# A last output and the next first tokens carried across a loop's back edge, with hints for its branch

## The chip, the core and the metric

The kernel runs on one core of one Trainium2 chip. The metric is the time of one execution on the device in microseconds (us), taken as the median of several runs. Before the change it is 9271.71 us, the median of 3 runs (9268.06 to 9273.82).

The engines are called as in the profile: PE is TensorE (PEld its weight loads), DVE is VectorE, ACT is ScalarE, POOL is GpSimd, SP is SyncE, which issues most DMA transfers. Each engine runs its own instruction stream, and each has its own copy of a loop's branch. A name with a q, such as PEldq, is the sequencer of that engine, which carries out branches, register loads and waits. L784 is line 784 of the kernel's file; the lines of the kernel before and after the change differ.

## The reference, cut to what matters

```
x = x + xattn(layernorm(x), ctx)         # 4 x 1024 tokens of 1024 values
h = layernorm(x).reshape(4096, 1024)
probs = softmax(h @ gate_w)              # 8 experts
topk_w, topk_idx = top_k(probs, 2)       # every token goes to 2 experts
topk_w = topk_w / sum(topk_w)
# for each expert e, on the tokens routed to it:
#   g = silu(h @ w1[e]) * (h @ w3[e])    # 1024 -> 3584
#   o = g @ w2[e]                        # 3584 -> 1024
out = x + sum over the 2 experts of topk_w * o
```

All of it is in float32. There are 4096 tokens and so 8192 pairs of token and expert, about 1024 for each of the 8 experts.

## The kernel before

**The parts.** The first 537 us hold the cross attention, the norms and the routing. They write the normed tokens to DRAM (`h_d`), write x into the output (`of`), put the ids and weights of each expert's tokens in a list (`id_d`), and fill a small table of *runs*: the expert of each run (`run_e`), its first slot in the list (`run_s`), its kind (`run_k`), and the number of runs (`run_n`). With this input there are 8 runs, one for each expert, of 3 blocks each, with widths of 328 to 360 tokens.

**The loop.** `tc.For_i(0, n_run)` at L784 goes over the runs; the number is read from memory. Its body reads the run's table entries into registers and jumps with `tc.Switch(kind, 13)` (L788) into one of 13 unrolled bodies, `run(i, ex, s0, blocks, width)` (L664), one for each kind in `RUNS`. At the end of a body every engine waits for its own work and for the others, and branches back. The order of PE's instructions in a body is the order in which the program is written (`manual_schedule`); a scheduler orders the other engines.

**One block** is `width` tokens, cut in `split` parts of up to 128 rows, the third part being 72 to 104 rows here.

- *Phase 1*: 14 steps `i2`, in each a tile of w1 and one of w3, 1 MB each, streamed by SP into three buffers (`load`, tag `w`). The products follow a scheme with seven half-size products p1 to p7 in place of eight: `weight_sums` (L573 to L577, four DVE operations) makes the sums of the weights' quarters, `token_sums` (L587) those of the tokens, the matmuls at L735 make the seven products (56 for one tile) in four PSUM banks, and `combine` (L599: a copy by ACT at L608, DVE at L610, 612, 613, 614) puts them together to c1 or c3. Then silu and a product give `g`.
- *Phase 2*: 4 column quarters q of w2, with matmuls at L766 and `combine` to `y`.
- *Tokens out* (`tokens_out`): for each part two transposes of y (L697) into PSUM and one accumulation into `acc` by DVE (L701); at the last quarter the three rows tiles are scattered to the output by POOL's indirect DMA (L707). `acc` is gathered from the output at the start of phase 2. The output of a quarter waits in a list `late` and is carried out after the first part of the next quarter's matmuls, or after the first tile of the next block; the last one of a run is carried out at the end of the body (`while late`, L779).
- *Tokens in* (`tokens_in`, L668): a copy of the ids, 24 transposes of the gathered rows (L679) in six PSUM tiles, copied to `x` by ACT (L687) and DVE (L685) in turn, and the token sums. It stands at the head of a run for its first block, and after the combine of quarter q = 1 for the next block of the same run.
- *Ahead of time*: `load_rows` (ids by SP, three gathers by POOL at L638) fetches the next block's rows at the start of a block. In the last block `load_first(i + 1)` (L749) does so for the next run, and loads its first two weight tiles to buffers of their own, w1a and w3a.

So a run of the loop ends with the last quarter's combine, its transposes, accumulation and scatters, and the next one begins, behind the branch and the switch, with the 24 transposes of its first tokens, four weight sums of w1a and then the first matmul at L735.

Of the kernel before, what the change touches and what calls it, by code (L numbers as in the profile page):

```python
# [18 lines left out]
P = 128  # L19
# [14 lines left out]
def kernel(  # L34
# [489 lines left out]


    with ExitStack() as st:
        fst = st.enter_context(tc.tile_pool(name="fst", bufs=1))
        wp = st.enter_context(tc.tile_pool(name="wp", bufs=3))
        ap = st.enter_context(tc.tile_pool(name="ap", bufs=1))
        hp = st.enter_context(tc.tile_pool(name="hp", bufs=1))  # L530
# [10 lines left out]
        HK = KD // 2  # L541
        NI = KM // 2


# [15 lines left out]

        def weight_sums(t, kn, halves):

            n = kn // 2
            if halves:
                v = t[:, :kn, :].rearrange("p (i h) c -> p i h c", h=2)
                lo, hi = v[:, :, 0, :], v[:, :, 1, :]
            else:
                lo, hi = t[:, :n, :], t[:, n:kn, :]
            a11, a21 = lo[:, :, :P], lo[:, :, P:]
            a12, a22 = hi[:, :, :P], hi[:, :, P:]  # L570
            s = wp.tile([P, 3, HK, P], F32, tag="s", name="ws")
            s1, s2, s4 = s[:, 0, :n, :], s[:, 1, :n, :], s[:, 2, :n, :]
            nc.vector.tensor_tensor(s1, a21, a22, ALU.add)  # L573
            nc.vector.tensor_tensor(s2, s1, a11, ALU.subtract)  # L574
            nc.vector.tensor_tensor(s4, a12, s2, ALU.subtract)  # L575
            s3 = a21
            nc.vector.tensor_tensor(s3, a11, a21, ALU.subtract)  # L577
            return dict(p1=a11, p2=a12, p3=s4, p4=a22, p5=s1, p6=s2, p7=s3)

# [18 lines left out]

        def combine(pp, n, tag):  # L599

            def pair(t):
                return t[:, : 2 * n].rearrange("p (a b) -> p a b", b=n)

            def twice(v):
                return v.unsqueeze(1).to_broadcast([P, 2, n])

            p1s = gp.tile([P, n], F32, tag="p1s", name="p1s")
            nc.scalar.copy(p1s, pp[0][:, :n])  # L608
            c = gp.tile([P, 4, n], F32, tag=tag, name=tag)
            nc.vector.tensor_tensor(c[:, 0:2, :], pair(pp[1]), twice(p1s), ALU.add)  # L610
            vu = gp.tile([P, 2, n], F32, tag="vu", name="vu")
            nc.vector.tensor_tensor(vu, pair(pp[2]), twice(c[:, 1, :]), ALU.add)  # L612
            nc.vector.tensor_tensor(c[:, 1:3, :], pair(pp[3]), vu, ALU.add)  # L613
            nc.vector.tensor_tensor(c[:, 3, :], pp[2][:, :n], vu[:, 1, :], ALU.add)
            return c

# [32 lines left out]
        w1a = fst.tile([P, KD, QW], F32, name="w1a")  # L649
        w3a = fst.tile([P, KD, QW], F32, name="w3a")  # L650

        def load_rows(s0):
# [5 lines left out]
        def load_first(i):  # L658
            ex = expert(i)
            load_rows(first_slot(i))  # L660
            weights(w1a, w1f, ex, 0, KD, 0)
            weights(w3a, w3f, ex, 0, KD, 0)

        def run(i, ex, s0, blocks, width):  # L664
            n = width // 2
            split = [min(P, width - c) for c in range(0, width, P)]

            def tokens_in():  # L668

                ids = ip.tile([P, RT, IDW], I32, tag="ids", name="ids")  # L670
                nc.vector.tensor_copy(ids, ids0)
                rd = ip.tile([P, RT], I32, tag="rd", name="rd")
                nc.vector.tensor_copy(rd, rd0)
                x = hp.tile([P, HK, 7 * n], F32, tag="x", name="x")
                for s, r in enumerate(split):
                    for h in range(2):
                        pt = pst.tile([P, N], F32, tag="pt", name="pt_h")
                        for k in range(HK):
                            nc.tensor.transpose(  # L679
                                pt[:, ts(k, r)], rows[s][:r, ts(HK * h + k, P)], ident[:r, :r]  # L680
                            )
                        src = pt[:, : HK * r].rearrange("p (a b) -> p a b", b=r)
                        dst = x[:, :, ds((B11 + 2 * h) * n + s * P, r)]
                        if h % 2:
                            nc.vector.tensor_copy(dst, src)  # L685
                        else:
                            nc.scalar.copy(dst, src)  # L687
                xv = x.rearrange("p k (q c) -> p k q c", q=7)
                token_sums(xv, n)
                return ids, rd, xv  # L690

            def tokens_out(ids, acc, q, y):
                yv = y.rearrange("p (d h) c -> p d (h c)", h=2)
                for s, r in enumerate(split):
                    pt = pst.tile([P, N], F32, tag="pt", name="pt_y")
                    for d in range(2):
                        nc.tensor.transpose(  # L697
                            pt[:r, ts(d, P)], yv[:, d, ds(s * P, r)], ident
                        )
                    part = acc[s][:r, ts(q, QW)]  # L700
                    nc.vector.scalar_tensor_tensor(  # L701
                        part, pt[:r, :QW], ids.bitcast(F32)[:r, s, 1:2], part,
                        ALU.mult, ALU.add,
                    )
                if q == DQ - 1:
                    for s, r in enumerate(split):
                        nc.gpsimd.indirect_dma_start(  # L707
                            out=of,
                            out_offset=bass.IndirectOffsetOnAxis(
                                ap=ids[:r, s, 0:1], axis=0  # L710
                            ),
                            in_=acc[s][:r, :],
                            in_offset=None,
                            bounds_check=T - 1,
                            oob_is_err=False,
                        )

            late = []
            now = tokens_in()
            for b in range(blocks):  # L720
                ids, rd, x = now
                last = b == blocks - 1
# [3 lines left out]
                for i2 in range(NI):  # L726
                    cs = []
                    for wf, wa, tag in ((w1f, w1a, "c1"), (w3f, w3a, "c3")):
                        t = load(wf, ex, 0, KD, i2 * QW) if b or i2 else wa
                        left = weight_sums(t, KD, False)  # L730
                        pp = banks()
                        for p in ORDER if b or i2 else EARLY:
                            bk, half = BANK[p]
                            for k in range(HK):
                                nc.tensor.matmul(  # L735
                                    pp[bk][:, ts(half, n)], left[p][:, k, :],
                                    x[:, k, RIGHT[p], :],
                                    start=(k == 0), stop=(k == HK - 1),
                                )
                        cs.append(combine(pp, n, tag))  # L740
                        while late:
                            late.pop(0)()
                    c1, c3 = cs
                    nc.scalar.activation(c1, c1, AF.Silu)  # L744
                    nc.vector.tensor_tensor(g[:, i2, B11 : B22 + 1, :], c1, c3, ALU.mult)  # L745
                    token_sums(g[:, i2, :, :], n)

                if last:
                    load_first(i + 1)  # L749
                acc = [  # L750
                    ap.tile([P, D], F32, tag=f"acc{s}", name="acc") for s in range(len(split))
                ]
                for s, r in enumerate(split):
                    gather(acc[s][:r, :], of, rd, s, r)
                for q in range(DQ):
                    pp = banks()
                    i2 = 0
                    for kn in W2K:
# [14 lines left out]
                        while late:  # L773
                            late.pop(0)()
                    y = combine(pp, n, "y")
                    late.append(lambda a=ids, c=acc, d=q, e=y: tokens_out(a, c, d, e))
                    if q == 1 and not last:
                        now = tokens_in()
            while late:  # L779
                late.pop(0)()  # L780

        load_first(0)
        n_run = nc.values_load(run_n, min_val=1, max_val=NRUN)
        with tc.For_i(0, n_run) as i:  # L784
            ex = expert(i)
            s0 = first_slot(i)
            kind = nc.values_load(run_k[:, ds(i, 1)], min_val=0, max_val=len(RUNS) - 1)
            for k in tc.Switch(kind, len(RUNS)):  # L788
                with tc.manual_schedule(engines={ENG.PE}):
                    run(i, ex, s0, *RUNS[k])  # L790


# [26 lines left out]
```

## Time and profile before

| | |
|---|---|
| median of 3 runs | 9271.71 us (9268.06 to 9273.82) |
| the profiled execution | 9277.28 us, its span 9275.4 us |
| mean granted clock of PE | 0.977 |
| PE busy | 8865.5 us, 96%, 59428 matmuls and transposes |
| PEld busy | 8665.9 us, 93% |
| DVE busy | 5115.8 us, 55%, 10003 instructions |
| ACT, POOL busy | 694.4 us (7%), 406.0 us (4%) |
| DMA | 1236.36 MB, mean 133 GB/s |
| matmuls of phase 1 (L735) | 3285.3 + 2571.8 us |
| matmuls of phase 2 (L766) | 2031.6 + 1619.6 us |
| transposes of tokens in (L679) | 98.3 us busy, 272.7 us idle just before them |
| weight tiles of 1 MB | 848, median 5.1 us from issue to landing |
| scatters to the output (L707) | 72, three a block |

The table gives busy time of each engine in one profiled execution. "Idle before" of a group of instructions is the time in which its engine did nothing just ahead of them. The span is what the profiler saw of the execution from its first to its last instruction; the execution's own time is 1.9 us longer. Granted clock is the share of TensorE's full clock that the throttle gave.

### The profile page before, as it was taken

How to read it: one execution, taken by the hardware profiler on the slowest of the kernel's cores; microseconds unless marked ns; L12 is line 12 of the kernel's file. 1: busy time of each engine (PE TensorE's matmuls, PEld its weight loads, DVE VectorE, ACT ScalarE, POOL GpSimd, SP SyncE). 2: the span in 40 equal slices, each digit the busy share in tenths (PEclk: the TensorE clock that was granted, in tenths of full speed). 3: DMA queues.
4: the chain of work that ended last, by engine and by line, in shares of the span. 5: the costliest groups of instructions: out<-in, count | busy, mean ns of one | idle time of the engine just before them, and what ended most of it. 6: DMA issues, size and time to landing. Idle time of an engine off the chain costs nothing. (4 is left out here: it accounts for less than half of the span.)

```text
span 9275.4 us, 139976 instructions
## 1 busy us (share of the span) xinstructions
PE 8865.5 (96%) x59428; PEld 8665.9 (93%) x59429; DVE 5115.8 (55%) x10003; ACT 694.4 (7%) x1524; POOL 406.0 (4%) x494
## 2 busy tenths in 40 slices
PE   8979998999989999899989999899998999989999
PEld 5569998999989999899989999899998999989999
DVE  5655654655645555556546556465564565555654
ACT  3300000000000000000000000000000000000000
POOL 2310000000000000000000000000000000000000
PEclk9979999999999999999999999999999999999999
DMA  3234444344433444344434434444443344434343
GB/s 132 109 123 145 138 144 141 125 147 130 157 118 118 143 131 138 119 136 138 141 128 135 139 121 138 132 132 146 137 147 120 125 140 135 141 117 141 124 134 127
DMA packets 1116668, 1236.36 MB, mean 133 GB/s; under 512 B 34848, under 2 KB 1077280, under 8 KB 1115872
## 3 DMA queue, kind: packets, MB, share of 16 engines
q1 hardware_dynamic: 1079424, 1114.54, 37.1%
q0 software_dynamic: 31952, 107.24, 3.3%
q8 instruction: 500, 8.19, 0.4%
q10 hardware_dynamic: 4496, 3.97, 0.1%
q14 instruction: 296, 2.42, 0.1%
HBM read 1155.26 MB, written 70.65 MB: 132 GB/s over the span
## 5 line engine op out<-in xcount | busy, mean ns | idle before, releaser
L735 PE MATMUL ps<-x,wt 128*128 128x168 f32 (+3 forms) x20992 | 3285.3, 309 | 0.0
L735 PEld LDWEIGHTS ps<-x,wt 128*128 128x128 f32 x20992 | 3123.4, 190 | 0.0
L735 PE MATMUL ps<-x,ws 128*128 128x168 f32 (+3 forms) x16128 | 2571.8, 309 | 0.0
L735 PEld LDWEIGHTS ps<-x,ws 128*128 128x128 f32 x16128 | 2411.8, 190 | 0.0
L766 PE MATMUL ps<-g,wt 128*128 128x168 f32 (+3 forms) x10752 | 2031.6, 310 | 0.0
L573 DVE TENSOR_TENSOR ws<-wt 128x512 f32<-128x512 f32 (+1 forms) x1040 | 693.8, 667 | 2206.3 <-DMA wt<-in_L_ffn_w_dram 2123.3
L766 PEld LDWEIGHTS ps<-g,wt 128*128 128x128 f32 x10752 | 1693.4, 191 | 0.0
L766 PE MATMUL ps<-g,ws 128*128 128x168 f32 (+3 forms) x8064 | 1619.6, 310 | 0.0
L766 PEld LDWEIGHTS ps<-g,ws 128*128 128x128 f32 x8064 | 1299.0, 191 | 0.2 <-DVE y L610 0.2
L610 DVE TENSOR_TENSOR c<-ps,p1s 128x352 f32<-128x352 f32 (+3 forms) x672 | 346.7, 516 | 1045.1 <-PE ps L735 1016.1
L574 DVE TENSOR_TENSOR ws<-ws,wt 128x512 f32<-128x512 f32 (+1 forms) x1040 | 692.4, 666 | 30.2
L577 DVE TENSOR_TENSOR wt<-wt 128x512 f32<-128x512 f32 (+1 forms) x1040 | 685.3, 659 | 0.0
L575 DVE TENSOR_TENSOR ws<-wt,ws 128x512 f32<-128x512 f32 (+1 forms) x1040 | 684.3, 658 | 0.0
L608 ACT COPY p1s<-ps 128x168 f32<-128x168 f32 (+3 forms) x768 | 228.5, 298 | 5319.3 <-PE ps L766 2881.0
L744 ACT ACTIVATE c<-c 128x672 f32<-128x672 f32 (+3 forms) x336 | 261.6, 778 | 2559.5 <-DVE c L613 2543.4
L613 DVE TENSOR_TENSOR c<-ps,vu 128x352 f32<-128x352 f32 (+3 forms) x672 | 344.6, 513 | 43.2 <-PE ps L735 36.2
L679 PE MATMUL pt_h<-ident,rows 128*128 128x128 f32 (+4 forms) x576 | 98.3, 319 | 272.7 <-DVE ws L573 128.4
L612 DVE TENSOR_TENSOR vu<-ps,c 128x352 f32<-128x352 f32 (+3 forms) x672 | 342.2, 509 | 17.5 <-PE ps L735 17.5
L679 PEld LDWEIGHTS pt_h<-ident,rows 128*128 128x128 f32 (+4 forms) x576 | 74.9, 169 | 295.0 <-issue 240.3
L745 DVE TENSOR_TENSOR g<-c,c 128x672 f32<-128x672 f32 (+3 forms) x336 | 294.1, 875 | 11.3
L638 POOL DMA_INDIRECT rows<-h_d,rd x75 | 78.1, 1042 | 4180.1 <-DVE ws L574 4136.0
L707 POOL DMA_INDIRECT out_dram<-acc,ids x72 | 74.0, 1028 | 4136.6 <-DVE acc L701 3929.3
(165 smaller groups left out, 3073.3 us busy)
## 6 DMA issues: line engine op xcount, KB each, us to landing
wt<-in_L_ffn_w_dram SPq DMA_DIRECT2D x848, 1024.0 KB, 5.1
wt<-in_L_ffn_w_dram SPq DMA_DIRECT2D x192, 768.0 KB, 4.7
xt<-in_x_dram SPq DMA_DIRECT2D x32, 512.0 KB, 4.4
out_dram<-x SPq DMA_DIRECT2D x32, 512.0 KB, 2.9
h_d<-hn SPq DMA_DIRECT2D x32, 512.0 KB, 2.6
w1a<-in_L_ffn_w_dram SPq DMA_DIRECT2D x9, 1024.0 KB
w3a<-in_L_ffn_w_dram SPq DMA_DIRECT2D x9, 1024.0 KB, 11.9
cx<-in_ctx_dram SPq DMA_DIRECT2D x4, 1024.0 KB, 9.9
```

The lines of the kernel that those rows point to most:

```text
L573: nc.vector.tensor_tensor(s1, a21, a22, ALU.add)
L574: nc.vector.tensor_tensor(s2, s1, a11, ALU.subtract)
L575: nc.vector.tensor_tensor(s4, a12, s2, ALU.subtract)
L577: nc.vector.tensor_tensor(s3, a11, a21, ALU.subtract)
L608: nc.scalar.copy(p1s, pp[0][:, :n])
L610: nc.vector.tensor_tensor(c[:, 0:2, :], pair(pp[1]), twice(p1s), ALU.add)
L612: nc.vector.tensor_tensor(vu, pair(pp[2]), twice(c[:, 1, :]), ALU.add)
L613: nc.vector.tensor_tensor(c[:, 1:3, :], pair(pp[3]), vu, ALU.add)
L735: nc.tensor.matmul(pp[bk][:, ts(half, n)], left[p][:, k, :], x[:, k, RIGHT[p], :], start=(k == 0), stop=(k == HK - 1),)
L744: nc.scalar.activation(c1, c1, AF.Silu)
L745: nc.vector.tensor_tensor(g[:, i2, B11 : B22 + 1, :], c1, c3, ALU.mult)
L766: nc.tensor.matmul(pp[bk][:, ts(half, n)], left[p][:, k, :], g[:, i2, RIGHT[p], :], start=(i2 == 0 and half == 0), stop=(i2 == NI - 1 and ...
```

## The change

- **Last output.** The last block's quarter q = 3 is combined into a tile `y1` that lives outside the loop, and the body ends there. A function `leftover()` does the tokens out of `y1` with ids kept in `ids1`: the next run puts it first in its `late` list, so it is carried out after the first weight tile's matmuls and combine, and once more behind the loop. It always takes three full tiles of 128 rows; the ids of rows beyond the block's width are put out of range (`beyond`), so that the scatter leaves them out. Ahead of the first run `acc` and `y1` are set to zero and `ids1` to an id out of range (`NONE`).
- **First tokens.** `tokens_in` stands after q = 1 of every block, the last one too, and once ahead of the loop. It always transposes three tiles of 128 rows. `x` lives outside the loop, is stored as two halves of contiguous tokens, and its sums (`xs`) are made by `token_factors(n)`, four DVE operations: in place for the blocks of a run, at the head of a run for its first block. The copies of ids (`take_ids`) are made at the head of each block.
- **First weight sums.** The sums of w1a are made in the last block of the run before, after its `tokens_in`, into `s1a` outside the loop; ahead of the loop for the first run.
- **Buffers.** `acc` lives outside the loop; `y` has one buffer in place of two.
- **Hints.** `For_i` gets `hint_engines` for the five engines.

The diff, cut to its core (`factors` and `weight_sums` now return the same products as before, with the buffer of the sums given from outside if wanted; `combine` writes into a given tile):

```diff
+        s1a = fst.tile([P, 3, HK, P], F32, name="s1a")
+        x = fst.tile([P, KD, XW], F32, name="x")
+        xs = fst.tile([P, HK, 3, NM], F32, name="xs")
+        ids1 = fst.tile([P, RT, IDW], I32, name="ids1")
+        nc.gpsimd.memset(ids1, NONE)
+        acc = [fst.tile([P, D], F32, name=f"acc{s}") for s in range(RT)]
+        for a in acc:
+            nc.gpsimd.memset(a, 0.0)
+        y1 = fst.tile([P, 2 * XW], F32, name="y1")
+        nc.gpsimd.memset(y1, 0.0)
...
+        def tokens_in():
+            for s in range(RT):
+                for h in range(2):
+                    pt = pst.tile([P, N], F32, tag="pt", name="pt_h")
+                    for k in range(HK):
+                        nc.tensor.transpose(
+                            pt[:, ts(k, P)], rows[s][:, ts(HK * h + k, P)], ident
+                        )
...
+        def token_factors(n):
+            b11, b12 = x[:, :HK, :n], x[:, :HK, n : 2 * n]
+            b21, b22 = x[:, HK:, :n], x[:, HK:, n : 2 * n]
+            t1, t2, t4 = (xs[:, :, j, :n] for j in range(3))
+            nc.vector.tensor_tensor(t1, b12, b11, ALU.subtract)
+            t3 = b12
+            nc.vector.tensor_tensor(t3, b22, b12, ALU.subtract)
+            nc.vector.tensor_tensor(t2, b22, t1, ALU.subtract)
+            nc.vector.tensor_tensor(t4, b21, t2, ALU.subtract)
+            return dict(p1=b11, p2=b21, p3=b22, p4=t4, p5=t1, p6=t2, p7=t3)
...
+        def leftover():
+            tokens_out(ids1, [P] * RT, DQ - 1, y1)
+
         def run(i, ex, s0, blocks, width):
...
-            late = []
-            now = tokens_in()
+            late = [leftover]
+            right = token_factors(n)
             for b in range(blocks):
-                ids, rd, x = now
+                ids, rd = take_ids()
...
-                        left = weight_sums(t, KD, False)
+                        if t is w1a:
+                            left = factors(w1a, KD, False, s1a)
+                        else:
+                            left = weight_sums(t, KD, False)
...
                 if last:
                     load_first(i + 1)
-                acc = [
-                    ap.tile([P, D], F32, tag=f"acc{s}", name="acc") for s in range(len(split))
-                ]
+                    beyond = ip.tile([P, RT], F32, tag="beyond", name="beyond")
+                    nc.vector.tensor_scalar(
+                        beyond, at, float(width), float(NONE), ALU.is_ge, ALU.mult
+                    )
+                    nc.vector.tensor_tensor(ids1[:, :, 0], beyond, ids[:, :, 0], ALU.add)
+                    nc.vector.tensor_copy(ids1[:, :, 1], ids[:, :, 1])
...
-                    y = combine(pp, n, "y")
-                    late.append(lambda a=ids, c=acc, d=q, e=y: tokens_out(a, c, d, e))
-                    if q == 1 and not last:
-                        now = tokens_in()
-            while late:
-                late.pop(0)()
+                    if last and q == DQ - 1:
+                        combine(pp, n, y1, XW)
+                        break
+                    y = gp.tile([P, 2 * XW], F32, tag="y", name="y", bufs=1)
+                    combine(pp, n, y, XW)
+                    late.append(lambda a=ids, d=q, e=y: tokens_out(a, split, d, e))
+                    if q == 1:
+                        tokens_in()
+                        if last:
+                            weight_sums(w1a, KD, False, s1a)
+                        else:
+                            right = token_factors(n)
 
         load_first(0)
+        tokens_in()
+        weight_sums(w1a, KD, False, s1a)
         n_run = nc.values_load(run_n, min_val=1, max_val=NRUN)
-        with tc.For_i(0, n_run) as i:
+        with tc.For_i(0, n_run, hint_engines=(ENG.PE, ENG.DVE, ENG.Activation, ENG.SP, ENG.Pool)) as i:
...
+        leftover()
```

In the changed kernel the matmuls stand at L776 (phase 1) and L815 (phase 2), the transposes of tokens in at L699, those of tokens out at L726 with the accumulation at L728 and the scatter at L733, and the loop at L841.

More of the change, by code (lines that the diff above doesn't have):

```diff
@@ L528 @@
         wp = st.enter_context(tc.tile_pool(name="wp", bufs=3))
-        ap = st.enter_context(tc.tile_pool(name="ap", bufs=1))
         hp = st.enter_context(tc.tile_pool(name="hp", bufs=1))
@@ L542 @@
         NI = KM // 2
+        NM = RUNS[-1][1] // 2
+        XW = RT * P
+        assert all(w // 2 <= NM and w <= XW for _, w in RUNS)
         T1, B11, B12, B21, B22, T2, T4 = range(7)
@@ L559, in load, with factors @@
             return t
-        def weight_sums(t, kn, halves):
+        def factors(t, kn, halves, s):
             n = kn // 2
@@ L568, in weight_sums @@
                 lo, hi = t[:, :n, :], t[:, n:kn, :]
[L569 to L578, printed above, removed]
+            s1, s2, s4 = (s[:, j, :n, :] for j in range(3))
+            return dict(
+                p1=lo[:, :, :P], p2=hi[:, :, :P], p3=s4, p4=hi[:, :, P:], p5=s1, p6=s2,
+                p7=lo[:, :, P:],
+            )
+        def weight_sums(t, kn, halves, s=None):
+            if s is None:
+                s = wp.tile([P, 3, HK, P], F32, tag="s", name="ws")
+            f = factors(t, kn, halves, s)
+            a11, a12, a21, a22 = f["p1"], f["p2"], f["p7"], f["p4"]
+            nc.vector.tensor_tensor(f["p5"], a21, a22, ALU.add)
+            nc.vector.tensor_tensor(f["p6"], f["p5"], a11, ALU.subtract)
+            nc.vector.tensor_tensor(f["p3"], a12, f["p6"], ALU.subtract)
+            nc.vector.tensor_tensor(a21, a11, a21, ALU.subtract)
+            return f
         RIGHT = dict(p1=B11, p2=B21, p3=B22, p4=T4, p5=T1, p6=T2, p7=T3)
@@ L597, in banks, with combine @@
             return [ps.tile([P, N], F32, tag="ps", name=f"ps{i}") for i in range(4)]
-        def combine(pp, n, tag):
+        def combine(pp, n, c, wide):
             def pair(t):
@@ L608, in combine @@
             nc.scalar.copy(p1s, pp[0][:, :n])
-            c = gp.tile([P, 4, n], F32, tag=tag, name=tag)
-            nc.vector.tensor_tensor(c[:, 0:2, :], pair(pp[1]), twice(p1s), ALU.add)
+            nc.vector.tensor_tensor(pair(c), pair(pp[1]), twice(p1s), ALU.add)
             vu = gp.tile([P, 2, n], F32, tag="vu", name="vu")
[L612 to L615, printed above, removed]
+            nc.vector.tensor_tensor(vu, pair(pp[2]), twice(c[:, n : 2 * n]), ALU.add)
+            mid = c[:, n : 2 * wide - n].rearrange("p (a b) -> p a b", b=wide - n)[:, :, :n]
+            nc.vector.tensor_tensor(mid, pair(pp[3]), vu, ALU.add)
+            nc.vector.tensor_tensor(
+                c[:, wide + n : wide + 2 * n], pp[2][:, :n], vu[:, 1, :], ALU.add
+            )
         def expert(i):
@@ L650 @@
         w3a = fst.tile([P, KD, QW], F32, name="w3a")
+        s1a = fst.tile([P, 3, HK, P], F32, name="s1a")
[8 more added lines that the diff above has]
+        nc.gpsimd.memset(y1, 0.0)
+        at_i = fst.tile([P, RT], I32, name="at_i")
+        nc.gpsimd.iota(at_i, pattern=[[P, RT]], base=0, channel_multiplier=1)
+        at = fst.tile([P, RT], F32, name="at")
+        nc.vector.tensor_copy(at, at_i)
         def load_rows(s0):
@@ L662, in load_first, with tokens_out @@
             weights(w3a, w3f, ex, 0, KD, 0)
+        def tokens_in():
[5 more added lines that the diff above has]
+                            pt[:, ts(k, P)], rows[s][:, ts(HK * h + k, P)], ident
+                        )
+                    src = pt.rearrange("p (a b) -> p a b", b=P)
+                    dst = x[:, ds(HK * h, HK), ts(s, P)]
+                    if h % 2:
+                        nc.vector.tensor_copy(dst, src)
+                    else:
+                        nc.scalar.copy(dst, src)
+        def token_factors(n):
[8 more added lines that the diff above has]
+            return dict(p1=b11, p2=b21, p3=b22, p4=t4, p5=t1, p6=t2, p7=t3)
+        def tokens_out(ids, split, q, y):
+            yv = y.rearrange("p (d c) -> p d c", d=2)
+            for s, r in enumerate(split):
+                pt = pst.tile([P, N], F32, tag="pt", name="pt_y")
+                for d in range(2):
+                    nc.tensor.transpose(pt[:r, ts(d, P)], yv[:, d, ds(s * P, r)], ident)
+                part = acc[s][:r, ts(q, QW)]
+                nc.vector.scalar_tensor_tensor(
+                    part, pt[:r, :QW], ids.bitcast(F32)[:r, s, 1:2], part, ALU.mult, ALU.add
+                )
+            if q == DQ - 1:
+                for s, r in enumerate(split):
+                    nc.gpsimd.indirect_dma_start(
+                        out=of,
+                        out_offset=bass.IndirectOffsetOnAxis(ap=ids[:r, s, 0:1], axis=0),
+                        in_=acc[s][:r, :],
+                        in_offset=None,
+                        bounds_check=T - 1,
+                        oob_is_err=False,
+                    )
+        def leftover():
+            tokens_out(ids1, [P] * RT, DQ - 1, y1)
         def run(i, ex, s0, blocks, width):
@@ L666, in run, with take_ids @@
             split = [min(P, width - c) for c in range(0, width, P)]
-            def tokens_in():
+            def take_ids():
                 ids = ip.tile([P, RT, IDW], I32, tag="ids", name="ids")
@@ L673, in tokens_in @@
                 nc.vector.tensor_copy(rd, rd0)
[L674 to L716, printed above, removed]
@@ L718, in run @@
-            late = []
-            now = tokens_in()
+                return ids, rd
+            late = [leftover]
+            right = token_factors(n)
             for b in range(blocks):
-                ids, rd, x = now
+                ids, rd = take_ids()
                 last = b == blocks - 1
@@ L736, in run @@
                                     pp[bk][:, ts(half, n)], left[p][:, k, :],
-                                    x[:, k, RIGHT[p], :],
+                                    right[p][:, k, :],
                                     start=(k == 0), stop=(k == HK - 1),
                                 )
-                        cs.append(combine(pp, n, tag))
+                        c = gp.tile([P, 4 * n], F32, tag=tag, name=tag)
+                        combine(pp, n, c, 2 * n)
+                        cs.append(c)
                         while late:
@@ L744, in run @@
                     nc.scalar.activation(c1, c1, AF.Silu)
-                    nc.vector.tensor_tensor(g[:, i2, B11 : B22 + 1, :], c1, c3, ALU.mult)
+                    nc.vector.tensor_tensor(
+                        g[:, i2, B11 : B22 + 1, :].rearrange("p a b -> p (a b)"), c1, c3,
+                        ALU.mult,
+                    )
                     token_sums(g[:, i2, :, :], n)
@@ L749, in run @@
                     load_first(i + 1)
-                acc = [
-                    ap.tile([P, D], F32, tag=f"acc{s}", name="acc") for s in range(len(split))
-                ]
+                    beyond = ip.tile([P, RT], F32, tag="beyond", name="beyond")
+                    nc.vector.tensor_scalar(
+                        beyond, at, float(width), float(NONE), ALU.is_ge, ALU.mult
+                    )
+                    nc.vector.tensor_tensor(ids1[:, :, 0], beyond, ids[:, :, 0], ALU.add)
+                    nc.vector.tensor_copy(ids1[:, :, 1], ids[:, :, 1])
                 for s, r in enumerate(split):
@@ L774, in run @@
                             late.pop(0)()
-                    y = combine(pp, n, "y")
-                    late.append(lambda a=ids, c=acc, d=q, e=y: tokens_out(a, c, d, e))
-                    if q == 1 and not last:
-                        now = tokens_in()
-            while late:
-                late.pop(0)()
+                    if last and q == DQ - 1:
[8 more added lines that the diff above has]
+                            weight_sums(w1a, KD, False, s1a)
+                        else:
+                            right = token_factors(n)
         load_first(0)
+        tokens_in()
+        weight_sums(w1a, KD, False, s1a)
         n_run = nc.values_load(run_n, min_val=1, max_val=NRUN)
-        with tc.For_i(0, n_run) as i:
+        with tc.For_i(0, n_run, hint_engines=(ENG.PE, ENG.DVE, ENG.Activation, ENG.SP, ENG.Pool)) as i:
             ex = expert(i)
```

## The prediction

> **What bounds the kernel now.** I read the page first: TensorE (PE) is busy 96% of the span, VectorE (DVE) 55%, so the time is the PE stream plus the places where it stands still. Of the idle time of PE after 500 us, nearly all lies ahead of line 679, the transposes of a run's tokens. So the second view is the stages, cut from the end of a run's last output matmul (L766) to the first matmul (L735) of the next, for the seven back edges of the eight runs:
>
> ```profile
> core 0: us, PE busy (x) PEld busy (x) DVE busy (x) ACT busy (x) POOL busy (x), PEclk, DMA share, GB/s
> 1568.10:1608.10 40.00, 6.20 (x31) 4.76 (x30) 8.05 (x18) 2.88 (x4) 7.13 (x7) 0.57 0.24 79
> ...
> 8142.90:8177.60 34.70, 6.41 (x31) 4.95 (x30) 8.09 (x18) 2.94 (x4) 7.28 (x7) 0.57 0.29 90
> sum 248.10, PE 44.36 PEld 34.09 DVE 56.91 ACT 20.43 POOL 50.92; mean PE 6.34 PEld 4.87 DVE 8.13 ACT 2.92 POOL 7.27
> ```
>
> Seven edges take 248 us, and PE has 44 us of work in them. Third, the timeline of the last edge says what fills it. The last matmul ends at 8142.88. Combine, transposes and accumulation end at 8145.7. Then three scatters run one after the other:
>
> ```profile
> 8144.94 1.01 POOL L707 DMA_INDIRECT out_dram<-acc,ids  x1 [136.90 <-DVE acc L701]
> 8151.67 1.00 POOL L707 DMA_INDIRECT out_dram<-acc,ids  x1 [5.72 <-DMA out_dram<-acc,ids]
> 8155.84 0.93 POOL L707 DMA_INDIRECT out_dram<-acc,ids  x1 [3.17 <-DMA out_dram<-acc,ids]
> 8169.61 0.19 DVE L671 COPY ids<-ids 128x48 int32<-128x48 int32 x1 [23.95 <-issue]
> ```
>
> The last scatter lands at 8159.4. The drain and two barriers at L784 end at 8165.0, and the jump into the right case of the switch ends at 8169.4 to 8170.0. Then come transposes until 8177.57. Fourth, the rows of the sequencers at the loop's lines (count: min/median/max in ns, first and last start in us):
>
> ```profile
> L784 PEldq COMPARE_BRANCH  x10: 96/4900/5196, 537.9 to 9272.4; - x10
> L815 PEldq BRANCH_PREFETCH_HINT  x8: 31/36/45, 538.2 to 8165.1; - x8
> L815 DVEq BRANCH_PREFETCH_HINT  x8: 50/50/61, 544.7 to 8165.1; - x8
> ```
>
> The back edge's branch costs PE 4.9 us, although hints stand in the loop already.
>
> **What is removed at the edge.** I write T for the end of a run's last L766 matmul. The new body ends with the combine into y1, whose last operation starts at T+0.36 (8143.24). DVE's way from the start of its last operation to its drain was 4.87 us (8145.18 to 8150.05, most of it the branch), so it arrives at T+5.2. PE has 0.1 plus 4.96 us of branch, T+5.1. POOL is long there: its scatters are gone, and its branch and its drain (2.36 us, once 7.82) lie beside the last matmuls; if they did not, they would cost up to 6 us an edge. I take T+5.4 for the last arrival. From there to PE's start of the body took 1.1 us (8164.00 to 8165.12), from there into the case 4.86 (8169.98), and the first matmul needs one wait: 5.4+1.1+4.9+0.2 = 11.6 us. Seven edges cost 81 instead of 248: a gain of 167. Bounds: 10 us an edge (ScalarE's branch, with no transfer beside it, took 3.1) to 13 (DVE's slowest 5.2, plus a slow switch).
>
> **The hints** cost and bring nothing: both programs have one hint for each of the five engines at the head of the body, and the same rows stand in the trace above.
>
> **What the same work costs inside the run.** *Tokens in.* Sixteen of these 24 blocks of transposes lie inside a run already, with PE's other work stopped, as the chain shows:
>
> ```profile
> 8450.83 20.89 PE ps L766 x140
> 8471.72 0.45 PE pt_h L679 x4
> ...
> 8476.60 8.38 PE ps L766 x56
> ```
>
> This one took 4.9 us. Over the 16, matmul to matmul, the sum is 77.4 us, and the time grows with the rows of the third tile: 4.45 at 72, about 4.65 at 80, 5.0 at 96 and 104. The new block always moves 128 rows, so I carry the slope of 0.02 us a row on: 5.3 us. The change has 24 of them in runs: 24x5.3-77 = 50 more, less 1 for the matmul that each interval holds. Six of the 16 were followed by a 3.4 us stretch at granted clock 0.5; at the same rate 3 more come, 1.7 us lost in each: 5. Together 54 (35 if 128 rows cost no more, 65 with the worst).
>
> *Tokens out.* 88 of these lie in runs, median 1.37 us; the leftover adds one to each run. But its place is new, and there I expect a wait. Behind the jump the order of DVE's queue in the changed kernel is: token factors, the first sums, the four sums of the first streamed weight tile, combine, then an operation that needs the **second** streamed tile, and only then the accumulation that frees the PSUM buffer for the third output transpose. PE's queue is fixed by hand, so everything behind that transpose waits. In the trace of before the same operation already waits, with nothing of PE behind it:
>
> ```profile
> 8185.40 0.53 DVE L610 TENSOR_TENSOR c<-ps,p1s 128x352 f32<-128x352 f32 x1 [0.70 <-PE ps L735]
> 8188.62 0.69 DVE L573 TENSOR_TENSOR ws<-wt 128x512 f32<-128x512 f32 x1 [2.70 <-DMA wt<-in_L_ffn_w_dram]
> ```
>
> It starts 18.8 us after SP's entry into the case (8169.78). By bytes moved, the second tile was complete 14.3 to 17.8 us after entry at the eight starts; SP's queue moved 0.35 MB/us alone and about 0.1 while POOL's gathers ran. In the changed kernel SP first loads the next run's registers (1.34 us in the trace), which puts all three tiles 1.3 us later. But the three acc gathers (1.5 MB) move behind the leftover, and only the three gathers of rows compete. SP's bytes start at about 4.7 us, POOL's at 7.6: 1.0 MB until then, 0.5 MB during the gathers (5.2 us), the rest of 2.1 MB at full rate: 14.6 us. Then 0.6+0.43+0.48 us on DVE: PE goes on at 16.2. PE arrives at about 11.8 (0.35 start, 8.35 for 56 passes of 0.149, 0.5 transposes, 2.6 half clock). A stall of 4.4, with the transposes 5.2 us in each of seven runs: 36, and 1.4 in the first, where SP enters long before PE. If the tile is early this is 1.4 each; if it takes 17.8, 8.4.
>
> *The clock.* PE idle for 2.1 us at 4164.9 was followed by a half-clock stretch, so a 4.4 us stall drops it too: one and a half stretches of 3.4, 2.1 us net of what is hidden, 15 for seven (0 to 18). At the edge itself the clock falls in both kernels. In before the transposes sat in the slow part and the first matmuls lost 1.05 us on average (0.4 to 3 us at half pitch ahead of the return); now matmuls take it all, 5.1 us at half speed, 2.6 lost: 1.55x7 = 11 (bounds 0 and 23, from stretches of 7.3 to 10.7 us after the restarts of before). The Trainium skill ("TensorE: Matmul & The Clock Gate", "What's actually happening") says one busy window of about 3.4 us brings the full clock back. By that this term would be 5, and the total 6 us lower; the trace took longer, though with gappy transposes.
>
> *Entry and exit.* Tokens of the first run now come ahead of the loop, so PE's register loads and its switch (3.43 us, hidden until now behind the first gather) follow its transposes: 5.5 us, plus a slower fetch beside the weight loads (DVE's took 6.6 there) and clock: 8 (5 to 12). The POOL memsets (0.32 us for 256 columns, so about 4 for all) end about when rd0 is ready, 544; nothing. The exit adds one set of 13 waits ahead of the last scatter: 0.5.
>
> **The sum.** 167 - 54 - 38 - 15 - 11 - 8 - 0.5 = 41 us. The profiled execution took 9277.3 us (span 9275.4); less 41 it is 9236. The median of the three runs lies 5.6 lower, so 9231.
>
> **Rivals.** *The second tile is early* (it lands by 11 us, before the gathers bite): stall and clock drop vanish, 27+15 us more, 9189. For it: the acc gathers are gone, and in three of eight starts SP's bytes began within 2.3 us. Against it: 14.3 us was the best so far. 0.20. *The starved tile* ends on the other side: every microsecond that the second tile is later costs 7. From 20.5 us after entry the change loses; beyond 23 it is over 0.2% slower, at 24 us 9297. For it: SP's queue got a quarter of the bandwidth beside POOL's, and all tiles are issued 1.3 us later; the third tile needed 20 to 21.5. Against it: half of POOL's bytes moved away. 0.11. *A wash*: edge and in-run terms both at their bad bounds, 9271. For it: 126 us of 167 are given back by my own count. 0.14. *The hints work now*: the 4.4 us of branch go, 31 more, 9200. The same rows before speak against it: 0.03. The Trainium skill ("Advanced Engine Details and Errata", "Control Flow Timing") gives about 108 ns for compare-and-branch, which the 4900 ns above contradict.
>
> **How the numbers follow.** 0.52 for the forecast; with the early tile and the hints, faster by over 0.2% (18.5 us, about what a measurement of this kernel can tell) has 0.75; within it 0.14 (the wash); slower 0.11. The range: 9170 takes in the early tile with tokens in at no more for 128 rows (19 less), 9274 the forecast with a late tile (+20), the slow clock (+12) and the rest of the way to the wash.
>
> **What would show it.** Right: the hints' rows as before, PE's branch at the loop's new line (L841) still near 4.9 us; 11.6 us from the last output matmul to the first L776 matmul; in each run but the first a PE gap of about 4 us ahead of the third L726 transpose, behind a DVE operation that waits for wt; 24 blocks of L699 at 5.3 us. Wrong: an edge over 15 us, no gap at L726, or tokens in far from 5.3.

## The result, and the profile after

The changed kernel takes 9156.85 us (median of 4 runs, 9153.83 to 9163.01), against 9272.76 us before in the same comparison (9268.06 to 9277.82). The ratio is 0.9876, with a 95% interval of 0.9859 to 0.9893: 116 us less. The prediction had the direction, but 41 us less, and its range ended at 9170.

The page of the changed kernel, its first two lines (busy time, share of the span, instructions):

```profile
span 9152.1 us, 139985 instructions
...
PE 8851.7 (97%) x59458; PEld 8653.8 (95%) x59459; DVE 5121.5 (56%) x10062; ACT 697.8 (8%) x1527; POOL 411.5 (4%) x503
```

The work of PE is the same within 14 us; the span is 123.3 us shorter. (These are two single executions, of 9277.28 and 9153.83 us; they lie 123 us apart where the medians lie 116 apart, so some 7 us of the 123 are the spread from one execution to the next.) So the time came from where PE stood still. The windows of the seven back edges, cut as before from the last output matmul of a run (now L815) to the first matmul of the next (now L776):

```profile
core 0: us, PE busy (x) PEld busy (x) DVE busy (x) ACT busy (x) POOL busy (x), PEclk, DMA share, GB/s
1576.45:1586.65 10.20, 0.01 (x1) 0.03 (x1) 0.85 (x4) 0.00 (x0) 0.00 (x0) 0.69 0.04 10
...
8039.73:8050.05 10.32, 0.00 (x1) 0.02 (x1) 1.62 (x4) 0.00 (x0) 0.00 (x0) 0.60 0.05 12
sum 73.25, PE 0.03 PEld 0.10 DVE 11.06 ACT 0.00 POOL 0.00; mean PE 0.00 PEld 0.01 DVE 1.58 ACT 0.00 POOL 0.00
```

73 us in place of 248, with nothing on PE, ACT and POOL in them. The scatters have left the edge. The hints' rows and the branch (count: min/median/max in ns) are what they were:

```profile
L841 PEldq COMPARE_BRANCH  x10: 96/4700/4937, 554.3 to 9136.5; - x10
L873 PEldq BRANCH_PREFETCH_HINT  x8: 31/36/45, 554.7 to 8045.1; - x8
L873 DVEq BRANCH_PREFETCH_HINT  x8: 50/50/61, 555.3 to 8045.1; - x8
```

What the prediction got wrong stands behind the jump. The timeline of DVE and PE at the head of the last run:

```profile
8060.18 0.53 DVE L620 TENSOR_TENSOR c<-ps,p1s 128x352 f32<-128x352 f32 x1 [0.65 <-issue]
8060.62 0.68 DVE L585 TENSOR_TENSOR ws<-wt 128x512 f32<-128x512 f32 x1
8061.22 0.52 DVE L622 TENSOR_TENSOR vu<-ps,c 128x352 f32<-128x352 f32 x1
8061.66 0.47 DVE L728 SCALAR_TENSOR_TENSOR acc<-pt_y,ids,acc 128x256 f32<-128x256 f32 x1
```

```profile
8061.12 0.60 PE L726 MATMUL pt_y<-ident,y 128*128 128x128 f32 x4
8062.19 0.44 PE L726 MATMUL pt_y<-ident,y 128*128 128x128 f32 x2 [0.47 <-DVE acc L728]
```

The order of DVE is the one the prediction read: combine (L620), the first sum of the second streamed tile (L585), then the accumulation (L728) that PE waits for. But L585 has no bracket: it waited for no DMA here. At five of the seven restarts (the starts of a run behind a back edge) it waited for none, at the other two for 0.30 and 0.59 us (the runs that start at 4808.1 and 6953.3 us). The gap on PE is 0.47 us here and 0.47 to 2.37 us over the seven restarts, not 4.4; what is left of it is DVE's own queue, the combine and the sums ahead of L728.

Cut by stage, from one profiled execution of each kernel (us, the minus sign is a gain):

| term | predicted | measured |
|---|---|---|
| seven edges | -167 | -174.8 (248.1 to 73.3) |
| phase 2: tokens in, with its slow stretches | +54 | +30.8 (+37.9 in the eight last blocks, -7.1 in the other sixteen) |
| leftover output and the stall in it | +38 | +19.2 (eight, matmul to matmul) |
| clock drops behind that stall, and the clock at the edge | +26 | +9.2 (rest of the +28.4 in the first blocks' phase 1) |
| phase 1 of the other blocks | 0 | -4.6 |
| entry | +8 | -0.2 |
| exit | +0.5 | -2.9 |
| sum | -41 | -123.3 |

### The profile page after: what moved, and what is told of

The parts are those of the page before. It is cut to its first block, busy times and chain, and to the rows that moved or that the text cites. A ratio compares the mean times of both kernels' runs of the same rounds, so it can differ in the third digit from the quotient of the medians.

```text
span 9152.1 us, 139985 instructions
## 1 busy us (share of the span) xinstructions
PE 8851.7 (97%) x59458; PEld 8653.8 (95%) x59459; DVE 5121.5 (56%) x10062; ACT 697.8 (8%) x1527; POOL 411.5 (4%) x503
## 5 line engine op out<-in xcount | busy, mean ns | idle before, releaser
L776 PE MATMUL ps<-x,wt 128*128 128x168 f32 (+3 forms) x15744 | 2510.4, 309 | 0.0
L776 PEld LDWEIGHTS ps<-x,wt 128*128 128x128 f32 x15744 | 2353.3, 190 | 0.0
L815 PE MATMUL ps<-g,wt 128*128 128x168 f32 (+3 forms) x10752 | 2027.2, 309 | 0.0
L585 DVE TENSOR_TENSOR ws<-wt 128x512 f32<-128x512 f32 (+1 forms) x1040 | 693.0, 666 | 2075.8 <-DMA wt<-in_L_ffn_w_dram 2028.2
L815 PEld LDWEIGHTS ps<-g,wt 128*128 128x128 f32 x10752 | 1688.6, 190 | 0.0
L776 PE MATMUL ps<-xs,ws 128*128 128x168 f32 (+3 forms) x10624 | 1659.1, 309 | 0.0
L815 PE MATMUL ps<-g,ws 128*128 128x168 f32 (+3 forms) x8064 | 1615.6, 309 | 1.4 <-DVE y L620 1.4
L776 PEld LDWEIGHTS ps<-xs,ws 128*128 128x128 f32 x10624 | 1579.0, 190 | 0.0
L815 PEld LDWEIGHTS ps<-g,ws 128*128 128x128 f32 x8064 | 1294.5, 190 | 1.9 <-DVE y L620 1.9
L620 DVE TENSOR_TENSOR c<-ps,p1s 128x352 f32<-128x352 f32 (+3 forms) x672 | 346.0, 515 | 1107.3 <-PE ps L776 1082.7
L776 PE MATMUL ps<-x,ws 128*128 128x168 f32 (+3 forms) x5312 | 884.0, 309 | 0.0
L776 PE MATMUL ps<-xs,wt 128*128 128x168 f32 (+3 forms) x5248 | 872.5, 309 | 0.0
L776 PEld LDWEIGHTS ps<-x,ws 128*128 128x128 f32 x5312 | 805.1, 190 | 0.0
L776 PEld LDWEIGHTS ps<-xs,wt 128*128 128x128 f32 x5248 | 794.3, 190 | 0.0
```

The lines of the kernel that those rows point to most:

```text
L585: nc.vector.tensor_tensor(f["p5"], a21, a22, ALU.add)
L620: nc.vector.tensor_tensor(pair(c), pair(pp[1]), twice(p1s), ALU.add)
L776: nc.tensor.matmul(pp[bk][:, ts(half, n)], left[p][:, k, :], right[p][:, k, :], start=(k == 0), stop=(k == HK - 1),)
L815: nc.tensor.matmul(pp[bk][:, ts(half, n)], left[p][:, k, :], g[:, i2, RIGHT[p], :], start=(i2 == 0 and half == 0), stop=(i2 == NI - 1 and ...
```

## The experiments

**The hints alone.** The change without its hints:

```diff
-        with tc.For_i(0, n_run, hint_engines=(ENG.PE, ENG.DVE, ENG.Activation, ENG.SP, ENG.Pool)) as i:
+        with tc.For_i(0, n_run) as i:
```

> The changed kernel without hint_engines. Theory (the hints bring nothing): 9157 us within 10, the seven edges 73 us as in the changed kernel, PE's branch back 4.6 to 4.9 us as there. Rival (the hints shorten the branches): each edge 2 to 4.4 us longer, 9171 to 9188 us.

Measured: 9159.1 us (9154.92 to 9160.83), against 9156.85 (9153.83 to 9163.01) with them; the edges sum to 72.7 us. The two programs have the same instructions, so this is also a second sample of the changed kernel, and its stages agree with the first within 3 us. The hints bring nothing.

**The last output alone.** The first tokens stay at the head of the run:

```diff
             late = [leftover]
+            tokens_in()
             right = token_factors(n)
...
-                            left = factors(w1a, KD, False, s1a)
+                            left = weight_sums(w1a, KD, False, s1a)
...
-                    if q == 1:
+                    if q == 1 and not last:
                         tokens_in()
...
         load_first(0)
-        tokens_in()
-        weight_sums(w1a, KD, False, s1a)
```

> Only the last output crosses the edge; the first tokens are taken in at the head of the run as before, with the sums of w1a. Theory (the scatters at the end of the body are nearly the whole gain; a set of transposes costs inside the run, 4.7 us, nearly what it saves at the edge, 7.5 us with a slow clock that the matmuls must otherwise bear): edges of about 18 us, 126 in all (53 more than the changed kernel), last blocks' phase 2 4.7 us shorter each (38 less), first matmuls of a run no longer at half clock (some 10 less): 9157 to 9170 us. Rival (both moves bring about half of the gain): about 9210 us.

Measured: 9148.36 us (9144.73 to 9152.87), even less than the whole change. Against the changed kernel the edges are 55.2 us longer (18.4 us an edge in place of 10.5), phase 2 is 37.1 shorter (4.6 in each last block), and phase 1 is 19.0 shorter (the matmuls at a run's start do not bear the slow clock, and the eight leftovers take 12.6 us in place of 19.2). In the loop that is 1 us. The rest of the difference lies ahead of it: from the arrival of the first rows to the first matmul 9.0 us in place of 11.2, and a routing part that was 6 us shorter. That last part is not touched by the change; its end lay between 491 and 501 us in the kernels of this study.

**The first tokens alone.** The last output is flushed at the end of the body as before:

```diff
-            late = [leftover]
+            late = []
...
-                    if last and q == DQ - 1:
-                        combine(pp, n, y1, XW)
-                        break
...
+            while late:
+                late.pop(0)()
...
-        leftover()
```

> Only the first tokens and w1a's sums cross the edge; the last output is flushed at the end of the body as before. Theory (as for the run with the last output alone): edges of 27 us, 190 in all (117 more than the changed kernel), no output transposes at the head of a run (18 less): about 9255 us, 17 less than before the change. Rival (both moves bring half): about 9215 us.

Measured: 9273.52 us, ratio to the kernel before 1.0001 (0.9992 to 1.0011): no difference. The edges (192.6 us) came as expected, 55.5 less than before the change; phase 2 takes 30.3 and phase 1 24.9 us more, which is all of it. The miss of 18 us is in phase 1: I had taken off the whole cost of the leftover, but blocks 1, 7 and 22 (of 24, counted from 0) each have a new stall of about 3 us ahead of an output transpose and a half-clock stretch behind it, 4 us in all each, and the slow clock at the edge stays. Why those three blocks, stays open.

So the two moves are far from equal: the last output, with its scatters, is the whole gain, the first tokens a wash as written.

**Where the stall went.** Three more gathers on POOL at the head of a run, into rows that are overwritten before use, and not waiting for the new ids:

```diff
+                if b == 0:
+                    for s in range(RT):
+                        gather(rows[s], h_d, rd, s, P)
                 if not last:
                     load_rows(s0 + (b + 1) * width)
```

> The changed kernel with three more gathers on POOL's queue at the head of each run (1.5 MB, rows that are overwritten before use), which do not wait for the new ids, so that POOL's transfers run beside the first streamed weight tiles as they did before the change. Theory (the stall that was predicted stays away because the second tile lands, 9.4 to 9.8 us after SP's entry, before POOL's first bytes at 9.4 to 9.6): second tile at 14 to 18 us, a PE gap of 4 to 8 us in place of 0.5 to 2.4 ahead of the third output transpose, half-clock stretches behind it: 9190 to 9215 us. Rival (the order of DVE alone sets the gap, the transfers do not matter): gap as before, 9157 to 9162 us.

Measured: 9197.2 us, ratio 0.9925 (0.9908 to 0.9941). What POOL's and SP's queues moved in the first 10 us behind SP's entry into the last run's case tells the three kernels apart (q1 is SP's queue, q0 POOL's; packets, MB, share). Before the change:

```profile
q1 hardware_dynamic: 1596, 1.23, 37.9%
q0 software_dynamic: 302, 1.12, 37.1%
```

The changed kernel:

```profile
q1 hardware_dynamic: 2501, 2.15, 65.5%
q0 software_dynamic: 59, 0.24, 5.9%
```

With three more gathers:

```profile
q1 hardware_dynamic: 1703, 1.34, 42.9%
q0 software_dynamic: 304, 1.13, 28.0%
```

In the changed kernel nearly all of both 1 MB tiles passes before POOL's bytes begin. With early gathers they share again, and the stall that the prediction described is there, with DVE's wait for the tile and PE's wait for DVE:

```profile
8095.65 0.69 DVE L585 TENSOR_TENSOR ws<-wt 128x512 f32<-128x512 f32 x1 [3.56 <-DMA wt<-in_L_ffn_w_dram]
```

```profile
8097.22 0.69 PE L726 MATMUL pt_y<-ident,y 128*128 128x128 f32 x2 [4.60 <-DVE acc L728]
```

Over the seven restarts the second tile was complete 13.2 to 15.0 us after entry (9.4 to 9.8 in the changed kernel), the gap was 3.7 to 6.3 us, and a half-clock stretch of 3.4 to 6.8 us followed each: phase 1 took 41 us more, 31 of them in the eight leftover outputs. The theory holds, and the rival (DVE's order alone) falls.

What starts POOL is seen in its timeline. Before, the first gather behind the jump is that of `acc`, which needs only the ids of a block long known:

```profile
8170.73 1.19 POOL L638 DMA_INDIRECT acc<-out_dram,rd  x1 [13.96 <-DVE ws L573]
...
8174.54 1.25 POOL L638 DMA_INDIRECT rows<-h_d,rd  x1 [1.35 <-issue]
```

Changed, `acc` must wait for the leftover's scatters, and `rows` is first, which needs ids that SP has only just fetched:

```profile
8054.26 1.21 POOL L650 DMA_INDIRECT rows<-h_d,rd  x1 [154.56 <-DVE ws L586]
...
8062.94 1.01 POOL L733 DMA_INDIRECT out_dram<-acc,ids  x1 [4.52 <-issue]
...
8078.01 0.97 POOL L650 DMA_INDIRECT acc<-out_dram,rd  x1 [3.03 <-DMA out_dram<-acc,ids]
```

It issues 4.6 us after SP's entry (before: 0.95), and its first packet starts another 4.6 us later (before: 1.9). Over the seven restarts of the changed kernel POOL's first packet starts 9.2 to 9.4 us after entry.

**The rows of the third tile.** The sets for a run's own next block with their real rows, as before:

```diff
-            for s in range(RT):
+            for s, r in enumerate(split):
...
-                            pt[:, ts(k, P)], rows[s][:, ts(HK * h + k, P)], ident
+                            pt[:, ts(k, r)], rows[s][:r, ts(HK * h + k, P)], ident[:r, :r]
...
-                        tokens_in()
+                        tokens_in() if last else tokens_in(split)
```

> The changed kernel, but the tokens of a run's second and third block are taken in with their real rows (third tile of 72 to 104 rows) as before the change; the next run's first tokens stay at 128 rows. Theory (the set waits for its copies out of PSUM, so rows of the third tile cost next to nothing): 9157 us within 8, 4.5 to 5.0 us a set. Rival 1 (0.02 us a row, as the prediction had it): 16 sets 0.4 to 1 us shorter each, about 9146 us. Rival 2 (smaller transposes leave PE idler and let its clock fall, as it did after 6 of 16 sets before the change): half-clock stretches of 3.4 us behind some of the 16 sets, about 9164 us.

Measured: 9152.33 us (9148.5 to 9157.31), spans 9152.8 and 9152.1: no difference that this can tell. The sets are 0.2 us shorter each (at a width of 328, 4.45 us at 72 rows and 4.68 at 128: 0.004 us a row; over the widths 0.003 to 0.010). The theory holds, and rival 1 falls. But 2 of these 16 were followed by a half-clock stretch, so the stretches of rival 2 are there, at too small a rate to show in the time. Over all kernels here with sets in one piece, such a stretch followed 8 of 32 sets with a smaller third tile (6 of 16 before the change, 2 of 16 here), and none of 144 sets of three full tiles.

**The leftover later.** After the first tile of step i2 = 2:

```diff
-                        while late:
+                        while late and (b or i2 > 1):
                             late.pop(0)()
```

> The changed kernel with the leftover output after the second step's weight tiles (i2 = 2) of a run in place of after the first tile. Theory (the gap ahead of the third output transpose, 0.5 to 2.4 us, is DVE's queue at a run's start): gap gone, 1.4 us a leftover, about 9149 us. Rival (the gap is the usual one of output transposes): 9157 us.

Measured: 9158.32 us (9152.54 to 9166.71), no gain. The eight leftovers took 22.8 us there, against 19.2. My reading of the gap as a matter of a run's start was wrong: a third output transpose waits for DVE's accumulation wherever the three stand together (97 such waits in the changed kernel's trace, 52.4 us in all).

**Tokens in, cut in three.** Instead of 24 transposes after q = 1, 8 behind each of the last three weight tiles of q = 2:

```diff
+                        if q == 2 and i2 > W2K[0] // 2 and i2 < NI + 1:
+                            tokens_in([TI.pop(0)])
...
-                    if q == 1:
-                        tokens_in()
+                    if q == 2:
```

> The changed kernel with the 24 transposes of tokens in cut in three, one part behind each of the last three weight tiles of quarter q = 2, so that no part needs a PSUM tile that is still being copied. Theory (a set costs 4.7 to 5.1 us because PE waits for copies; 8 transposes without a wait take 0.95 us): 2.9 us a block, 24 x 2 = 48 us less, about 9109 us. Rival (the copies then delay DVE's weight sums, and PE waits there): 9130 us or more.

Measured: 9106.16 us, ratio 0.982 (0.9804 to 0.9837). The chain of a set in the changed kernel shows what it removes:

```profile
8347.86 0.45 PE pt_h L699 x4
8348.31 0.02 issue
8348.33 0.59 ACT x L707
8348.93 0.04 issue
8348.97 0.67 PE pt_h L699 x4
8349.65 0.02 issue
8349.67 0.59 ACT x L707
```

There are two PSUM tiles for six groups, so PE waits for a copy of 0.59 us (ACT) again and again. Eight transposes at a time find both tiles free: 1.01 us a part.

**Everything cut in three.** Tokens in a part after each of q = 0, 1, 2, and tokens out, the leftover included, a part after each of three weight tiles (`tokens_out` returns one step for each part; `if late` in place of `while late`):

```diff
-                        while late:
+                        if late:
                             late.pop(0)()
...
-                    late.append(lambda a=ids, d=q, e=y: tokens_out(a, split, d, e))
-                    if q == 1:
-                        tokens_in()
+                    late += tokens_out(ids, split, q, y)
+                    if q < RT:
+                        tokens_in([q])
+                    if q == RT - 1:
```

> The changed kernel with tokens in cut in three (a part after each of the quarters q = 0, 1, 2) and tokens out, the leftover included, cut in three, one part after each of three weight tiles. Theory: tokens in as in the run with these alone (48 us less), tokens out 0.8 us in place of 1.54 us on average, 96 sets: 70 us less; about 9040 us. Rival (tokens out are hidden in part already, or each cut costs a change of matmul shapes): 9080 to 9110 us.

Measured: 9028.39 us, ratio 0.9738 (0.9722 to 0.9755), the fastest of all. The groups of transposes on PE between 1500 us and 9100 (changed) or 9000 us (this kernel): busy, mean ns | idle before, releaser. The changed kernel:

```profile
L726 PE MATMUL pt_y<-ident,y 128*128 128x128 f32 (+3 forms) x510 | 86.8, 279 | 44.9 <-DVE acc L728 44.9
L699 PE MATMUL pt_h<-ident,rows 128*128 128x128 f32 x528 | 78.0, 281 | 29.9 <-ACT x L707 28.3 <-DVE x L705 0.9
```

Everything in three:

```profile
L729 PE MATMUL pt_y<-ident,y 128*128 128x128 f32 x514 | 98.2, 273 | 0.0
L699 PE MATMUL pt_h<-ident,rows 128*128 128x128 f32 x515 | 66.9, 273 | 0.0
```

The idle time ahead of both is gone.

**The same, with a run's first tokens at its head.** The edit is that of the last output alone, on the kernel just above.

> The kernel with everything cut in three (e8_spread_all), but a run's first tokens are taken in at the head of the run, as in the run with the last output alone. There (e2) moving the tokens cost 9 us, with sets of 4.9 us inside the run. Theory (what decides is the price of a set inside the run against 7.9 us at the edge, less a slow clock of about 2 us that the matmuls must then bear): a set in three parts costs 2.6 us, so the move now pays; edges 55 us longer in all, eight sets inside the run less (21), matmuls at full clock at a run's start (16): about 9046 us, 18 slower than e8. Rival (the tokens are better at the head of the run whatever a set costs): 9020 us or less.

Measured: 9047.83 us (9045.44 to 9050.95). In the loop, against everything cut in three: edges 54.9 us more, phase 2 21.0 less, phase 1 16.1 less, so 17.8 more. The rival falls. A move that was a wash with a set of 4.9 us inside the run pays 18 us with one of 2.6.

## Why the prediction was wrong, point by point

- **Hints**: right. The rival "the hints work now" falls.
- **The edge**: right in kind, 10.2 to 10.9 us in place of 11.6. The end of DVE's way was over-charged: its branch went out 0.8 us after the last output matmul and its drain came at 4.2 to 4.5, not 5.2. PE's branch left 2.1 to 2.4 us ahead of the end of its last matmul, so half of its 4.7 us were hidden.
- **The stall**: the step that failed. The rule of the sum was "SP's bytes start at about 4.7 us, POOL's at 7.6: 1.0 MB until then", which put the second tile at 14.6 us and a stall of 4.4 us into each of seven runs, with a clock drop behind it. The starting times were wrong, on both sides. SP's bytes started at 3.3 to 3.5 us and POOL's at 9.2 to 9.4; SP's queue ran alone for about 5.9 us in place of 2.9, and 2.1 MB went, nearly all of both tiles. The second was complete at 9.4 to 9.8 us. I had the order right (`acc` behind the leftover, only `rows` in competition), but took the 4.7 from starts with another order: it is what SP took before the change where POOL's `acc` gather went first (4.6 to 5.0 us at three starts; 2.0 to 2.7 at the other four restarts). And I gave the gather of `rows` too little time: it issued at 4.5 to 4.7 us, but its first packet started 4.6 us after that. So the rival "the second tile is early" came true, which I gave 0.20; its own time, 9189, was still 32 us too long, and that rest lies in the other terms. The mechanism itself is real: it cost 40 us in the run with early gathers.
- **The clock behind the stall** went with it. At the edge 11 us were forecast; after the restart matmuls ran at half clock for 2.8 to 5.4 us, 4.0 on average, not 5.1, and what is left of the first blocks' extra, 9.2 us, holds this and one stretch inside a run. The Trainium skill ("TensorE: Matmul & The Clock Gate", "What's actually happening") gives one busy window of about 3.4 us for the clock's return, by which the term would have been 5. The 4.0 us of this trace lie between that and the 5.1.
- **Tokens in**: the slope of 0.02 us a row was for the most part the width of the block in disguise. In the kernel before, blocks with more rows in their third tile are also wider; with 128 rows everywhere the sets still take 4.7 us at widths 328 and 336, and 5.0 to 5.2 at 352 and 360; the rows themselves cost 0.003 to 0.010 us each. (Nor is 5.3 what the slope gives: 0.02 a row from 4.45 at 72 would be 5.6 at 128.) And the slow stretches that I carried on at 6 in 16 did not continue: full tiles had none. The two together are about the 23 us between 54 and 31.
- **Entry and exit**: from the arrival of the first rows to the first matmul it took 11.2 us in place of 6.7, so 4.5 of the 8 were there; the routing ahead of it ended 4.7 us earlier in this execution, which is no merit of the change. The exit gained 2.9 us where I had 0.5 against; its cause was not tried.

Put together, the lesser stall and clock (36 us), tokens in (23), the edge (8), entry and exit (12) and the other blocks' phase 1 (5) make the 83 us that the forecast was short.

## What to carry to other kernels

Before charging a moved transfer with contention, list which transfer on the competing queue goes first *after* the change and what it waits for, and take the starting times from starts with that same order: a gather that loses its early start can clear the way for a load that nothing else touched. A piece of work moved across a loop's back edge is worth its place there less its price inside the body; cut it so that it never needs more PSUM tiles than are free, and the same move goes from nothing to 18 us. Look first at what stands one behind the other at the edge: moving the last output, whose three scatters landed one after another (14.5 us of the last edge before, 8144.9 to 8159.4), was the whole gain here. The scatters alone were not moved in any run.

## What the runs showed of the hardware that was not expected

- Small tiles can cost clock. A half-clock stretch followed 8 of the 32 sets of transposes with a smaller third tile, and none of 144 sets of three full tiles. How much of a window PE was busy does not tell the two apart. In the kernel before, a window with 2.18 of 3.40 us busy (1891.0 to 1894.4) was followed by such a stretch; in the changed kernel one with 1.94 of 3.42 us (5468.11 to 5471.53), in a set of full tiles, was not. What counts instead stays open.
- How soon a gather's first packet starts after POOL issued it depends on the start. In the changed kernel it was 4.6 us at the last restart (8054.26 and 8058.9), in the kernel before 1.9 us (8170.73 and 8172.6). Over the 77 restarts in the eleven traces it was 1.9 to 2.2 us in the four where POOL's first packet came ahead of SP's first weight packet (three before the change, one with early gathers), and 3.0 to 5.4 us in the other 73. Why stays open.
- A branch that takes 4.7 us on PE's sequencer need not cost them: in the changed kernel it went out more than 2 us ahead of the end of PE's queued matmuls. Adding or leaving out the hints' argument changed neither the instructions nor the time.
